# Settling transposes, two split slots and one set of low parts, moved in a transformer block on one core

## The chip, the core and the metric

The kernel runs on one core of a Trainium2 chip. The metric is the device time of one execution in microseconds (us); lower is better. A core has five engines that this text names: TensorE (PE in the profile; its weight loads are PEld), VectorE (DVE), ScalarE (ACT), GpSimd (POOL) and SyncE (SP, which issues DMAs here).

## What is computed

The reference is one block of a perceiver on 32 sequences of 64 tokens of 512 features, all in float32, with three residual layers. Cut to what matters here:

```python
x = x + xattn(layernorm(x), ctx_2048, mask)          # cross attention, 256 context tokens
x = x + attn(layernorm(x), wq_a, wq_b, wkv_a, wkv_b, wo, ...)   # latent attention, 16 heads
r = layernorm(x)
routing = top_k(r @ gate_w, 2)
h = square(relu(r @ up_w))                           # 512 -> 2048
y = h @ down_w + (r @ expert_weight) * routing.sum()
x = x + layernorm(y) * ln_gamma + ln_beta
```

## The kernel before, in words

A float32 product is made of three matmuls of a faster format: each operand is split into a high part `hi` (a rounded copy, made by ScalarE) and a low part `lo = x - hi` (made by VectorE), and hi*hi, hi*lo and lo*hi are added up in PSUM. `split` (L144) is that pair of instructions, and a `pins` argument tells behind which instructions the two are to be queued on their engines.

The three large products, `wo` (the attention's way out), `up` and `down`, use a recursive scheme that makes seven products of eight. For that, sums of weight blocks are made on GpSimd ahead of time (`prep_sums`) and stored in DRAM. Each large weight is cut into eight pieces, k = 0 to 7, used in the order `ORDER = (0, 1, 5, 6, 7, 2, 3, 4)`. Each has a slot in SBUF. `read_slot(k, what)` (L644) loads a piece of `wo`, `up` or `down` into its slot, and `put_slot(k, what, pins)` (L652) splits it there: two copies on ScalarE and two subtractions on VectorE, the first 1024 elements wide, the second 768.

The stages follow one another on TensorE. First come the cross attention and the latent attention (to about 550 us of the profiled execution). Then the way out (`seven`, L723 to L726, tile `op`) runs over eight token blocks of 256, with the expert's product (`o_expert`, tile `cpe`) and transposes (`o_t`, tile `ops`) of earlier blocks between. The way up (`up_seven`, matmuls on L1156, tile `up`) runs over four blocks of 512 tokens, b = 0 to 3, with eight rounds each, n = 0 to 7, one per weight piece; a round is 42 matmuls of 256 columns. The way down (`seven` again, tile `dp`) runs over units of a token block and a weight piece, u = 0 to 63, 21 matmuls each.

A round of the way up writes four PSUM banks. `combine` (L158 to L168) adds them up into a tile `uo`: a copy on ScalarE (L160) and five additions on VectorE, the last of which, L168, reads the last bank. Two sets of banks alternate, so round n + 2 needs the banks that round n's `combine` frees. Then ScalarE applies Relu and Square (L1226, L1227), and the result is stored in DRAM (`h_d`) and read back for the way down, where `left` splits it (tile `hl`).

The right operand of the way up is the features of a block, `xr[b, part]`. Parts 0 and 2 are high parts (copies on ScalarE, L1067) and parts 1 and 3 are the low parts of 0 and 2 (two subtractions on VectorE, L1065). `right(b, part)` makes one. For block 1 they are made in rounds of block 0: `PARTS_FIRST` maps m = n - 3 to the parts made at the end of that round.

`settle(n, ps, ...)` (L709) issues n transposes into a PSUM bank whose content isn't used. With `behind=None` nothing but the bank and their operands holds them back. In the way down four of them are chained behind the last matmul of the unit before (at the units in `SETTLE_AT`, L1359).

The order of the instructions on each engine is made when the program is built: a scheduler takes instructions in the order in which they are traced, as soon as a cost model says that they are ready, and `after(ins)` (`issue_after`) forces everything in its block behind `ins` on that engine. Memory that a closed pool leaves is given to the tiles of later pools, which wait until the earlier tile was last used. The pool `o_act` (tiles `beb`, `mo`, `xt`, `oo`, and others, in the order of their first allocation) gives its memory to the first tiles `uo` of the way up and to the rooms of the features behind them.

Of the kernel before, what the change touches and what calls it, by code (L numbers as in the profile page):

```python
# [9 lines left out]
FP = mybir.dt.float32  # L10
# [8 lines left out]
P = 128  # L19
B, S, D = 32, 64, 512  # L20
# [9 lines left out]
NB = (B * S) // TB  # L30
# [11 lines left out]
ORDER = (0, 1, 5, 6, 7, 2, 3, 4)  # L42
# [2 lines left out]


XR = "hxhx"
PARTS_FIRST = {1: (0, 1), 2: (2,)}
PARTS = {1: (0,), 2: (1,), 3: (2,)}

BARE_FIRST, BARE_LAST = ORDER[:5], ORDER[2:]
# [35 lines left out]
def perceiver_block(ctx: ExitStack, tc: tile.TileContext, x, mem, mask, wq_a, bq_a, qnw, wq_b, bq_b,  # L87
                    wkv_a, bkv_a, kvnw, wkv_b, wo, bo, gate, up, down, expert, gamma, beta, cs, out):
    nc = tc.nc
# [51 lines left out]
    def after(ins):  # L141
        return tc.issue_after(ins.ins) if ins is not None else ExitStack()
# [32 lines left out]
    def mm3(ps, pairs):  # L175

        n = len(pairs)
        for j, (ah, al, bh, bl) in enumerate(pairs):
            nc.tensor.matmul(ps, ah, bh, start=(j == 0), stop=False)  # L179
            nc.tensor.matmul(ps, al, bh, start=False, stop=False)  # L180
            nc.tensor.matmul(ps, ah, bl, start=False, stop=(j == n - 1))  # L181


    with ExitStack() as mla:
# [25 lines left out]
        with ExitStack() as pa:  # L210
# [304 lines left out]
            for i in range(NT + 2):  # L515
# [37 lines left out]
                if i < NT:  # L553
                    xT = a_xT(i)
# [446 lines left out]

    def o_expert(blk, xh, xl, _):

        mo = mos.pop(blk, None) or ap.tile([P, 2, D], FP, tag="mo", name=f"mo{blk}")
        for tt in range(2):
            i = 2 * blk + tt
            sl = slice(tt * P, (tt + 1) * P)
            pes = []
            for c in (slice(256, NE), slice(0, 256)):
                pe = ps_t.tile([P, D], FP, tag="T", name=f"cpe{i}_{c.start}")  # L1010
                mm3(pe[:, 0 : c.stop - c.start], [
                    (xh[:, k, sl], xl[:, k, sl], wes[0][:, k, c], wes[1][:, k, c]) for k in range(NKD)
                ])
                pes.append(pe)
            t8 = sp.tile([P, 8], FP, tag="t8", name=f"t8{i}")
            nc.vector.max(t8, pes[0][:, 256:264])
            gs = sp.tile([P, 1], FP, tag="gs", name=f"gs{i}")
            nc.vector.tensor_tensor(gs, t8[:, 0:1], t8[:, 1:2], ALU.add)
            if tt:
                yield  # L1020
            nc.scalar.mul(mo[:, tt, 256:512], pes[0][:, 0:256], gs)
            nc.scalar.mul(mo[:, tt, 0:256], pes[1][:, 0:256], gs)
        nc.scalar.dma_start(mo_d[blk], mo)
        yield

    xr, xc, xw = {}, {}, []

    def read_x(b, kk, room=None, behind=None):

# [37 lines left out]
                    ins = nc.scalar.copy(t[:, to], src)  # L1067
        return ins

    mos = {0: ap.tile([P, 2, D], FP, tag="mo", name="mo0")}  # L1070
    put_slot(ORDER[2], "wo")
    xt, xns, xT, x2s, dones, read = {}, {}, {}, {}, {}, 5
    for u, (blk, k) in enumerate(out_units):
# [61 lines left out]
    xT = o_t(NB - 1, xns.pop(NB - 1), lambda: next(scaled))  # L1135
    for part in range(3):
        right(0, part, (dones[NB - 1][0], xT[2][1]))
    put_slot(ORDER[2], "up", pins=xT[2])
    for _ in o_expert(NB - 1, *xT):
        pass  # L1140
    pc.close()


# [2 lines left out]
    with ExitStack() as pu:  # L1146
# [3 lines left out]
        def up_seven(ps, k, b, n, steps):  # L1150
            wh, wl = (t[:, 0:7].rearrange("p a (k f) -> p a k f", k=2) for t in wts[k])

            def product(s, parts, first=False, last=False):
                i, j = SEVEN[s]
                for m, (kk, w, low) in enumerate(parts):
                    nc.tensor.matmul(  # L1156
                        ps[s // 2][:, s % 2], w[:, i, kk], xr[b, 2 * kk + low][:, j],
                        start=(first and m == 0), stop=(last and m == len(parts) - 1),
                    )

            most = [(0, wh, 0), (0, wl, 0), (0, wh, 1), (1, wh, 0), (1, wl, 0)]
            rest = [(1, wh, 1)]
            one, two = (0, 2, 4, 6), (1, 3, 5)
            late = None
            if n == 0:
                with after(settle(8, ps, wh[:, 0, 0], ident2, None) if b == 0 else None):
                    for s in one:
                        product(s, most, first=True)
            if n == 7:
                for s in one:  # L1170
                    product(s, rest, first=True)
                for s in (0, 2, 4):
                    product(s, most, last=True)
                for s in two:
                    product(s, rest, first=True)
                if b + 1 < NB // 2:
                    late = right(b + 1, 3)
            for s in range(7):
                if n == 0 and s in one:
                    product(s, rest, last=True)  # L1180
                elif n < 7:
                    product(s, most + rest, True, True)
                elif s in two or s == 6:
                    product(s, most, last=True)
                if s in (1, 3, 5, 6):
                    with after(late if s == 3 else None):
                        next(steps)
# [8 lines left out]
                nc.sync.dma_start(h_d[b][:, k, 3:7], w)  # L1196

        stores = []
        right(0, 3)
        behind = read_slot(ORDER[5], "up", behind=reads[-1])  # L1200
        for b in range(NB // 2):
            if b == NB // 2 - 1:
                first = [(blk, k) for ks in (ORDER[:5], ORDER[5:]) for blk in DOWN[:2] for k in ks]
                out_units[:] = first + [(blk, k) for blk in DOWN[2:] for k in ORDER]
            for n, k in enumerate(ORDER):
                m = n - 3 if b == 0 else n - 1
                summed = None
                if 0 < b < NB // 2 - 1 and m in (0, 1):
                    read_x(b + 1, m)
                if b == 0 and n in (1, 2):  # L1210
                    behind = read_x(1, n - 1, x_room(1, n - 1), behind)
                if b == 0 and n in (0, 1):
                    behind = read_slot(ORDER[n + 6], "up", behind=behind)
                if b == NB // 2 - 1 and 0 < n < 7:
                    read_slot(ORDER[n - 1], "down")
                if b == NB // 2 - 1 and n == 4:
                    read_home(2, from_h, None)
                if b == NB // 2 - 1 and n in (5, 6):
                    read_pair(n - 2, from_h)
                ps = banks(ps_f[n % 2], f"up{b}_{k}")  # L1220
                o = fp.tile([P, 5, TB], FP, tag="o", name=f"uo{b}_{k}")
                p1 = fp.tile([P, TB], FP, tag="p1", bufs=2, name=f"up1_{b}_{k}")
                done = []
                up_seven(ps, k, b, n, combine(p1, ps, o, done))
                for q in (slice(0, 2), slice(2, 4)):
                    nc.scalar.activation(o[:, q], o[:, q], AF.Relu)  # L1226
                    act = nc.scalar.activation(o[:, q], o[:, q], AF.Square)  # L1227
                pins = (act, done[-1])
                o4 = o[:, 0:4].rearrange("p (c t) (a n) -> p c t a n", c=2, a=2)
                w = None  # L1230
                if not bare(b, k):
                    w = ccp.tile([P, 8, P], FP, tag="c", name=f"uw{b}_{k}").rearrange("p (d t) n -> p d t n", t=2)
                    at = [o4[:, i, :, a] for i in range(2) for a in range(2)] + [w[:, d] for d in range(4)]
                    summed = sums(at, LEFT)
                if b == 0 and n < 5:
                    put_slot(ORDER[n + 3], "up", pins=pins)
                if b == NB // 2 - 1 and 1 < n < 7:
                    put_slot(ORDER[n - 2], "down", pins=pins)
                if b == NB // 2 - 1 and n == 2:
                    for u in range(2):  # L1240
                        read_home(u, from_h, None)
                if b == NB // 2 - 1 and n == 3:
                    left(0, pins=(done[0], done[-1]))
                if b == NB // 2 - 1 and n == 5:
                    left(1, pins=(done[0], done[-1]))
                if b == NB // 2 - 1 and n == 6:
                    left(2, pins=(done[0], done[-1]))
                if b == NB // 2 - 1 and n == 7:
                    read_pair(5, from_h)
                if stores and (b, n) != (NB // 2 - 1, 7):  # L1250
                    store_h(*stores.pop(0))
                stores.append((b, k, o4, w))
                if b + 1 < NB // 2:
                    if m in (0, 1):
                        sum_x(b + 1, m, summed)
                    for q in (PARTS_FIRST if b == 0 else PARTS).get(m, ()):
                        right(b + 1, q, pins)

    with ExitStack() as pd:
# [82 lines left out]
        for u, (blk, k) in enumerate(out_units):  # L1342
# [23 lines left out]
                store_h(*stores.pop(0))  # L1366
            if u == 6:
                nc.sync.dma_start(gab, gamma.partition_broadcast(P))
            if u in (4, 6, 8):
                put_slot(ORDER[3 + u // 2], "down")  # L1370
            if u in (2, 4):
                read_slot(ORDER[5 + u // 2], "down")
            outs = [d for d in outs if step(d, low)]
# [52 lines left out]
```

## Time and profile before

| | us |
|---|---|
| median of 3 runs | 1103.69 |
| the three runs | 1099.43, 1103.69, 1105.27 |
| the profiled execution | 1098.9 |
| its span, first to last instruction | 1096.7 |
| its granted TensorE clock | 0.998 |

| engine | busy us | share of the span | instructions |
|---|---|---|---|
| PE | 1066.9 | 97% | 10201 |
| DVE | 769.0 | 70% | 1369 |
| ACT | 546.1 | 50% | 1051 |
| POOL | 508.1 | 46% | 691 |

The span is one execution, taken by the hardware profiler. In the timeline, a row is a start, a duration, an engine, a line of the kernel, an operation, the tiles written and read, their shapes and a count of merged instructions; in square brackets stands how long the engine had been idle and what ended that. In a table of windows a row is a stretch, its length, the busy time of the engine with the number of instructions, the granted clock, the mean busy share of the DMA engines and the GB/s that they moved. Matmuls overlap: one lasts 0.28 us and the next starts before it ends.

### The profile page before, as it was taken

The page shows a single profiled execution, that of the slowest core. Times are in us where ns is not written, and L with a number is a line of the kernel's source. Part 1 is how long each engine was busy: PE and PEld are TensorE (multiplying, and loading weights), DVE is VectorE, ACT ScalarE, POOL GpSimd, SP SyncE. Part 2 cuts the span into 40 slices and gives each one's busy share as a digit, 9 for nine tenths or more (in the row PEclk, how much of TensorE's full clock was granted, in tenths as well). Part 3 has the DMA queues.
Part 4 walks back from the last instruction along what each step waited for, and adds up shares of the span by engine and source line. Part 5 has one row for each costly group of instructions (what it writes and reads, how often), then busy time and mean ns, then how long its engine had stood idle before and what let it go on. Part 6 is the DMA issues. An engine that isn't in the chain of part 4 may idle for free.

```text
span 1096.7 us, 26072 instructions
## 1 busy us (share of the span) xinstructions
PE 1066.9 (97%) x10201; PEld 983.6 (90%) x10201; DVE 769.0 (70%) x1369; ACT 546.1 (50%) x1051; POOL 508.1 (46%) x691
## 2 busy tenths in 40 slices
PE   8999999999999999999998999999999999999996
PEld 6667777679999999999988999999999999999996
DVE  5666666657666666656787866667785658898786
ACT  4444444533433444434475544445676567755553
POOL 2333333326788778874570000003238970065671
PEclk9999999999999999999999999999999999999999
DMA  8867666343776778655487776779646689998672
GB/s 259 263 216 231 206 212 203 124 161 121 260 234 245 260 247 294 249 207 195 160 324 276 263 241 213 231 235 359 218 156 202 221 247 366 310 309 257 206 232 79
DMA packets 195386, 254.67 MB, mean 232 GB/s; under 512 B 18544, under 2 KB 140032, under 8 KB 195264
## 3 DMA queue, kind: packets, MB, share of 16 engines
q1 hardware_dynamic: 190704, 240.92, 67.0%
q10 hardware_dynamic: 3456, 8.39, 2.2%
q0 software_dynamic: 1104, 3.70, 0.9%
q8 instruction: 80, 1.31, 0.5%
q14 instruction: 42, 0.34, 0.1%
HBM read 146.67 MB, written 106.30 MB: 231 GB/s over the span
## 4 chain that ended last, share of the span: by engine, by line
PE 59%; DMA 10%; POOL 9%; DVE 8%; issue 7%; ACT 5%; SPq 1%; DVEq 0%; POOLq 0%; ACTq 0%
PE up L1156 9%; PE pss L773 5%; PE psq L179 4%; PE psq L180 4%; PE psq L181 4%; PE op L725 3%; PE op L726 3%; PE op L723 3%; PE psv L817 3%; DMA hd<-uo 2%; PE pse L179 2%; PE pse L181 2%; PE pse L180 2%; DMA x1d<-xt 2%; DMA vd<-vw 2%
## 5 line engine op out<-in xcount | busy, mean ns | idle before, releaser
L755 DVE SCALAR_TENSOR_TENSOR qe<-pse,bqp,cq 64x256 f32<-64x256 f32 x256 | 123.7, 483 | 76.5 <-PE pse L181 70.7
L1156 PE MATMUL up<-xr,wh_up 128*128 128x256 f32 x896 | 157.6, 280 | 0.6 <-DVE uo L168 0.6
L1156 PEld LDWEIGHTS up<-xr,wh_up 128*128 128x128 f32 x896 | 137.5, 189 | 1.0 <-issue 0.7
L725 PE MATMUL op<-wh_wo,hl 128*128 128x256 f32 x448 | 124.4, 279 | 3.7 <-DVE hl L149 3.7
L723 PE MATMUL op<-wh_wo,hl 128*128 128x256 f32 x448 | 124.0, 280 | 0.6 <-ACT hl L147 0.6
L725 PE MATMUL dp<-wh_down,hl 128*128 128x256 f32 x448 | 124.5, 278 | 0.0
L723 PE MATMUL dp<-wh_down,hl 128*128 128x256 f32 x448 | 124.4, 278 | 0.0
L726 PE MATMUL dp<-wl_down,hl 128*128 128x256 f32 x448 | 124.3, 277 | 0.0
L149 DVE TENSOR_TENSOR hl<-c,hl 128x896 fp32r<-128x896 f32 x84 | 94.3, 1126 | 42.3 <-ACT hl L147 42.0
L1156 PE MATMUL up<-xr,wl_up 128*128 128x256 f32 x448 | 123.7, 280 | 0.0
L726 PE MATMUL op<-wl_wo,hl 128*128 128x256 f32 x448 | 123.5, 277 | 0.0
L147 ACT CAST hl<-c 128x896 fp32r<-128x896 f32 x84 | 79.0, 942 | 77.7 <-PE op L726 38.0
L179 PE MATMUL psq<-qa_hi,qh 128*128 128x256 f32 x384 | 112.5, 293 | 0.0
L180 PE MATMUL psq<-qa_hi,ql 128*128 128x256 f32 x384 | 106.4, 277 | 0.0
L181 PE MATMUL psq<-qa_lo,qh 128*128 128x256 f32 x384 | 106.2, 276 | 0.0
L725 PEld LDWEIGHTS op<-wh_wo,hl 128*128 128x128 f32 x448 | 84.3, 188 | 4.8 <-DVE hl L149 4.7
L723 PEld LDWEIGHTS op<-wh_wo,hl 128*128 128x128 f32 x448 | 83.6, 188 | 1.5 <-ACT hl L147 0.8
L723 PEld LDWEIGHTS dp<-wh_down,hl 128*128 128x128 f32 x448 | 84.6, 189 | 0.0
L725 PEld LDWEIGHTS dp<-wh_down,hl 128*128 128x128 f32 x448 | 84.1, 188 | 0.4 <-DVE hl L149 0.4
L1156 PEld LDWEIGHTS up<-xr,wl_up 128*128 128x128 f32 x448 | 84.2, 188 | 0.0
L726 PEld LDWEIGHTS op<-wl_wo,hl 128*128 128x128 f32 x448 | 84.1, 188 | 0.0
L726 PEld LDWEIGHTS dp<-wl_down,hl 128*128 128x128 f32 x448 | 84.1, 188 | 0.0
(233 smaller groups left out, 3146.6 us busy)
## 6 DMA issues: line engine op xcount, KB each, us to landing
c<-vd SPq DMA_DIRECT2D x58, 448.0 KB, 4.2
cx<-in_ctx SPq DMA_DIRECT2D x32, 512.0 KB, 4.6
vd<-vw SPq DMA_DIRECT2D x29, 512.0 KB, 3.6
hd<-uo SPq DMA_DIRECT2D x107, 128.0 KB, 3.3
hd<-uw SPq DMA_DIRECT2D x21, 512.0 KB, 3.3
dcw<-hd SPq DMA_DIRECT2D x18, 448.0 KB, 5.6
vd<-v SPq DMA_DIRECT2D x30, 256.0 KB, 3.5
wd_wo<-pw_wo SPq DMA_DIRECT2D x8, 896.0 KB, 4.9
```

The source lines that it names most:

```text
L147: copy = nc.scalar.copy(hi, src)
L149: return copy, engine.tensor_tensor(lo, src, hi.bitcast(FP), ALU.subtract)
L179: nc.tensor.matmul(ps, ah, bh, start=(j == 0), stop=False)
L180: nc.tensor.matmul(ps, al, bh, start=False, stop=False)
L181: nc.tensor.matmul(ps, ah, bl, start=False, stop=(j == n - 1))
L723: first = nc.tensor.matmul(ps[s // 2][:, s % 2], h[:, a], wh[:, b], start=(k == 0 and s % 2 == 0), stop=False)
L725: nc.tensor.matmul(ps[s // 2][:, s % 2], l[:, a], wh[:, b], start=False, stop=False)
L726: ins = nc.tensor.matmul(ps[s // 2][:, s % 2], h[:, a], wl[:, b], start=False, stop=last)
L755: rope = nc.vector.scalar_tensor_tensor(qe[64 * a : 64 * a + 64, :], pe[r, :], bqp[r, p : p + 1], cq[r, a, :], ALU.add, ALU.mult,)
L773: nc.tensor.matmul(ps[64 * j : 64 * j + 64, pj, b, :], qs[2 * pj + j][a][:, sl], kT[:, a, kt], start=(a == 0), stop=(a == 1),)
L817: nc.tensor.matmul(o, kv[a, i, :], t[a, bp, :], start=True, stop=True)
L1156: nc.tensor.matmul(ps[s // 2][:, s % 2], w[:, i, kk], xr[b, 2 * kk + low][:, j], start=(first and m == 0), stop=(last and m == len(parts) ...
```

## The change

Five edits:

- The settling transposes ahead of the way up are four instead of eight, and they are pinned behind the last matmul of the last expert product (`ends`, for which `mm3` now returns its last matmul).
- `mo`, the expert's result, is no longer allocated ahead of the loop, so its place in `o_act` comes behind the tiles that are allocated earlier.
- `put_slot(ORDER[2], "up")` moves from before the last expert product to behind `right(0, 3)`, with its subtractions pinned behind that. `put_slot(ORDER[3], "up")` moves from the end of round 0 to the same place.
- In the last block of the way up, `put_slot(ORDER[4], "down")` moves from the end of round 6 to unit 0 of the way down, pinned behind the last Square and the last L168 of the way up.
- Block 1's part 1 (the low parts of its first features) is made at the end of round 5 of block 0 instead of round 4.

```diff
-PARTS_FIRST = {1: (0, 1), 2: (2,)}
+PARTS_FIRST = {1: (0,), 2: (1, 2)}
...
-            nc.tensor.matmul(ps, ah, bl, start=False, stop=(j == n - 1))
+            ins = nc.tensor.matmul(ps, ah, bl, start=False, stop=(j == n - 1))
+        return ins
...
-        mo = mos.pop(blk, None) or ap.tile([P, 2, D], FP, tag="mo", name=f"mo{blk}")
+        mo = ap.tile([P, 2, D], FP, tag="mo", name=f"mo{blk}")
...
-                mm3(pe[:, 0 : c.stop - c.start], [
+                made.append(mm3(pe[:, 0 : c.stop - c.start], [
                     (xh[:, k, sl], xl[:, k, sl], wes[0][:, k, c], wes[1][:, k, c]) for k in range(NKD)
-                ])
+                ]))
...
-    xr, xc, xw = {}, {}, []
+    xr, xc, xw, made = {}, {}, [], []
...
-    mos = {0: ap.tile([P, 2, D], FP, tag="mo", name="mo0")}
     put_slot(ORDER[2], "wo")
...
-    put_slot(ORDER[2], "up", pins=xT[2])
     for _ in o_expert(NB - 1, *xT):
         pass
+    ends = made[-1]
     pc.close()
...
-                with after(settle(8, ps, wh[:, 0, 0], ident2, None) if b == 0 else None):
+                with after(settle(4, ps, wh[:, 0, 0], ident2, ends) if b == 0 else None):
...
-        right(0, 3)
+        put_slot(ORDER[2], "up", pins=(xT[2][0], right(0, 3)))
+        put_slot(ORDER[3], "up", (xT[2][0], None))
...
-                if b == 0 and n < 5:
+                if b == 0 and 0 < n < 5:
                     put_slot(ORDER[n + 3], "up", pins=pins)
-                if b == NB // 2 - 1 and 1 < n < 7:
+                if b == NB // 2 - 1 and 1 < n < 6:
                     put_slot(ORDER[n - 2], "down", pins=pins)
...
-            if u in (4, 6, 8):
-                put_slot(ORDER[3 + u // 2], "down")
+            if u in (0, 4, 6, 8):
+                put_slot(ORDER[max(4, 3 + u // 2)], "down", pins=pins if u == 0 else (None, None))
```

## The prediction

> **What bounds the kernel now.** I read the page first: engines, then the granted clock.
>
> ```profile
> PE 1066.9 (97%) x10201; PEld 983.6 (90%) x10201; DVE 769.0 (70%) x1369; ACT 546.1 (50%) x1051; POOL 508.1 (46%) x691
> ...
> PEclk9999999999999999999999999999999999999999
> ```
>
> TensorE (PE) is busy for 97% of the span and the granted clock is full in every slice, so only two things can move the end: gaps in PE's stream, and the distance from one matmul's start to the next. A "busy" PE hides the second, since matmuls overlap. So I counted instructions in stretches of 20 us in the middle of the way up (windows, PE alone).
>
> ```profile
> 785.00:805.00 20.00, 20.00 (x172) 1.00 0.45 126
> 815.00:835.00 20.00, 20.00 (x179) 1.00 0.72 237
> 860.00:880.00 20.00, 20.00 (x172) 1.00 0.66 220
> ```
>
> All are 100% busy at clock 1.00, with the same matmuls (L1156, 256 columns), yet one holds 179 and the others 172. A matmul lasts 0.28 us, so some 2.4 of the count are the overlap at the edges: 20/176.5 is 113.3 ns apart, 20/169.7 is 117.8. The starts in the timeline say the same everywhere behind 560 us: 113.33 or 117.78 ns, nothing between for long. I call them the quick and the slow pace; 4.45 ns apart, 3.8% of PE time. Following the starts, the slow stretches behind 560 us are 560-576, 585-611, 773-809, 847-943 and 1036-1065 us. The pace changes only where PE is interrupted. At 808.87:
>
> ```profile
> 808.87 0.48 PE L1156 MATMUL up<-xr,wh_up 128*128 128x256 f32 x2 [0.57 <-DVE uo L168]
> ```
>
> slow before, quick after. Three late starts at 846.8-847.5 (258, 242 and 222 ns) do the reverse. Of the waits whose after-pace can be read, about as many end quick as slow. A row of transposes is another matter: each row of eight (L985) from 625 to 744 us and each row of four settling ones (L713, at 943.5 out of the slow pace, at 1008.3 out of the quick) is followed by the quick pace. Ahead of the way up:
>
> ```profile
> 764.82 1.08 PE L985 MATMUL ops<-ident,on 128*128 128x128 f32 x8 [1.02 <-DVE on L139]
> 765.75 0.49 PE L713 MATMUL up<-ident,wh_up 128*128 128x128 f32 x3
> 766.66 0.51 PE L179 MATMUL cpe<-we_hi,oh 128*128 128x264 f32 x2 [0.43 <-ACT oh L147]
> 767.01 0.60 PE L713 MATMUL up<-ident,wh_up 128*128 128x128 f32 x4
> ...
> 773.04 0.27 PE L713 MATMUL up<-ident,wh_up 128*128 128x128 f32 x1
> 773.07 0.36 PE L1156 MATMUL up<-xr,wh_up 128*128 128x256 f32 x1
> ```
>
> Seven of the eight settling transposes run ahead of the expert's matmuls; one stands where it was meant, and the way up starts slow. Last, VectorE (DVE) ahead of the stall at 808.87, and its hole at the start of the way up:
>
> ```profile
> 780.10 0.69 DVE L162 TENSOR_TENSOR uo<-up,up 128x512 f32<-128x512 f32 x1 [4.67 <-ACT up L160]
> ...
> 804.29 2.10 DVE L149 TENSOR_TENSOR wl_up<-wl_up,wh_up 128x1024 fp32r<-128x1024 f32 x2 [0.32 <-ACT wh_up L147]
> 806.30 0.96 DVE L1065 TENSOR_TENSOR xr<-xp,xr 128x768 fp32r<-128x768 f32 x1
> 807.17 1.23 DVE L1065 TENSOR_TENSOR xr<-xc,xr 128x1024 fp32r<-128x1024 f32 x1
> 808.30 0.42 DVE L168 TENSOR_TENSOR uo<-uo,up 128x256 f32<-128x256 f32 x1
> ```
>
> L168 frees the last bank of the sixth weight of block 0; the eighth weight needs it four matmuls after its start. It is late because the low part of block 1's features (L1065, 2.1 us) stands ahead of it. In the five rounds before, one round of DVE is five combining steps (2.6 us) and two low halves of a slot (2.1 us): 4.73 us from one L168 to the next (787.38, 792.11, 796.84, 801.57). A round of 42 matmuls takes 4.95 us slow and 4.76 quick: at the quick pace DVE has no room.
>
> **The change, part by part**, against the profiled execution's 1098.9 us (span 1096.7).
>
> *Pinned transposes.* Eight become four in a row behind the last expert matmul. Three of the eight lay in PE's 0.43 us wait and cost nothing; five stood on the path; now four do, at 109 ns: -0.1 us. If the row works as the rows at 625-744, 943.5 and 1008.3 did, the 302 matmuls from 773.07 to 808.87 come 4.45 ns closer: -1.35 us. Nothing is queued behind the pin but the way up itself, which needs the expert's end anyway.
>
> *Features' low parts apart.* The two L1065 move one round later, behind L168 and away from a slot's low halves. The stall's starts were 851 and 194 ns after their predecessors instead of 113: -0.82 us. They are needed where block 1 starts, some 811 us; behind L168 of the sixth round they end near 809. ScalarE's (ACT's) part of that round (L1067, 1.9 us) does not move. Next late would be L168 of the seventh round, pushed by 2.1 us; its bank is needed a whole round later, so it is covered.
>
> *One slot more ahead; rooms.* ORDER[3]'s split (ACT 1.8 us, DVE 2.1 us) leaves DVE's first round and goes to 770-774, where ACT is free until the scaling at 772.57 and DVE waits for the expert's last matmul before right(0, 3). ORDER[2]'s low halves go behind right(0, 3), into the hole that ends at 780.10; they are due at 782.6. Both slots landed before 767 us and the puts issue no DMA, so the SP and POOL queues keep their order. Behind ACT's two extra casts stand the expert's scalings and their store, at most 1.8 us later. That store mattered: mo's room lay under the first `uo`, and it landed at 779.97, just before L162 at 780.10, though its matmuls were done near 777.1. With mo allocated last, that room is that of tiles done earlier, and the first combine starts up to 2.8 us sooner. PE did not wait for it (bank due at 783.0), so 0 now; this pays for the quick pace: without it the rounds' 4.73 us would run into 4.76 us. If the cover failed, one stall like the present one, 0.8 us, and the pace open again.
>
> *One slot in the way down.* ORDER[4]'s split leaves 933.8-937.0 and goes behind the last Square and the last L168. Without its casts (1.67 us of ACT) ahead, the last Square ends at 938.6 instead of 940.2, or a us sooner if the casts of hl step behind it; then casts 1.77 us and the last low half 1 us: 940.3 to 941.4. The way down's fifth unit, which multiplies by it, is due at 931.05 + 84 x 0.1178 = 940.95. Behind it on both engines stand units' hl and slots ORDER[5], ORDER[6]; the low of the seventh unit ended at 946.3, when PE took it. So the price lies between 0 and about 2 us in small stalls; I take +0.4, nearer the low end, since DVE's own L168 comes 2 us earlier for it and both engines' work in that stretch stays the same.
>
> *Behind 809.* In the profiled execution 809-847 was quick already: 0 there. But all three timed runs (1099.43 to 1105.27) lie above the profiled one, so a typical run has more slow stretches; half of 38 us x 3.8% is -0.65 for the median run. The waits at 846.8 come from POOL's sums and the later right parts of block 1, which the change does not touch; I expect them again, with the pace afterwards open.
>
> Sum for a median run: -0.1 - 1.35 - 0.82 - 0.65 + 0.4 = -2.5 us, on 1103.69: **1101.2**. On the profiled execution, without the half, -1.9: 1097.0.
>
> [...]
>
> **Rivals.** (1) *All of the way up quick.* The waits at 847 vanish or come out quick, and block 2's likewise. Block 2 took 39.57 us, block 3 39.46, where 336 x 113.33 is 38.08: -2.87; block 1's tail -0.17; the way down's first 105 matmuls -0.47. With -2.5 that is -6.0: 1097.7; on the profiled run, with -1.9, -5.4: 1093.5. For it: block 1 ran quick for seven rounds. Against: its eighth round stalled just at that pace, and each stall is a coin.
>
> (2) *The row does nothing here*, or a stall in the first rounds undoes it. Then only -0.1 - 0.82 + 0.4: with no stall at 808.87 nothing brings the quick pace back, and 38 us of block 1 turn slow, +1.4 on the profiled run. So +0.9 for a run whose block 1 was quick and -0.5 for one where it was slow already, +0.2 between them: 1103.9. For it: the one row of four at 557.5 was slow again three us later, after a wait.
>
> (3) *Slower: the late split at the head of the way down.* ACT is full from 931.7 to 945.4. If ORDER[4]'s casts come out behind the seventh unit's cast (943.49, 0.94 us), they end at 946.2, the low half at 947.3, and the fifth unit waits 6.3 us; the units behind it then find their operands late, and the pace after the settling is lost until 1008 (62 us x 3.8% = 2.3). -2.5 - 0.4 + 6.3 + 2.3 = +5.7: 1109.4. It decides from a wait of some 3 us on. For it: the pin on the last Square; against: the split is traced ahead of that cast.
>
> **How the numbers follow.** Forecast case 0.45, rival 1 0.25, rival 2 0.15, rival 3 0.15. A measurement here tells about 0.5%, 5.5 us. The runs scatter by some 3 us on either side, from pace alone. Faster by more: 0.2 of the forecast case, 0.8 of rival 1, 0.1 of rival 2: 0.31. Slower by more: 0.05, none, 0.1, 0.9: 0.17. The rest, 0.52, is no change. The range reaches from below rival 1 (1097.7 less the scatter, and the profiled run's 1093.5) to rival 3's 1109.4: 1093 to 1109.
>
> **What the changed profile would show.** Right: four L713 in one row behind the last cpe, starts of L1156 113.33 ns apart from there, 179 matmuls in 785-805; no wait near 806; L162 of the first round near 777.3; ORDER[3]'s low halves before right(0, 3); the split of ORDER[4] done by 941 and no PE wait over 0.3 us in the fifth unit. Wrong: 172 in that window; a wait for `xr` or a slot in the first four rounds; a wait of PE for wl_down at the fifth unit. What I can't see is how the four changed orders shift the scheduling of each engine elsewhere; a stall in a place that I took as untouched would break the sum.

## The result, and the profile after

The median of 20 runs is 1105.18 us (1102.85 to 1109.99); the kernel before, run beside it, has 1102.24 us over 20 runs. The ratio is 1.0035, 95% interval [1.0021, 1.0049]: slower by 3.9 us of 1102.24 (the two medians differ by 2.9), where 2.5 us less was forecast. The profiled execution of after is the slowest of its 20 (1109.99 us, span 1108.2), that of before was one of the fastest of its kernel (1098.9), so the two traces differ by more than the medians do; what follows from a trace alone is said so. In the experiments one execution, the profiled one of the first kernel with the late place alone, took 3691.59 us with its matmuls some 0.41 us apart; its trace is not read, and that kernel was run a second time.

On the page, PE is as busy as before and the clock looks full (`PEclk` has a digit for each of 40 slices of the span):

```profile
PE 1072.0 (97%) x10197; PEld 986.5 (89%) x10197; DVE 770.3 (70%) x1369; ACT 545.3 (49%) x1051; POOL 508.0 (46%) x691
PEclk9999999999999999999999999999999999999998
```

PE has four instructions less and 5.1 us more of busy time. The three windows of the way up (PE alone; start and end, length, busy time with the count, clock, DMA share, GB/s) show where the count is lost:

```profile
785.00:805.00 20.00, 19.76 (x168) 1.00 0.38 107
815.00:835.00 20.00, 17.09 (x132) 0.91 0.66 216
860.00:880.00 20.00, 20.00 (x172) 1.00 0.65 211
```

The first window should have had 179 and has 168; the second had 179 before and has 132, with PE idle for 2.9 us and the clock cut. Ahead of the way up, in the timeline of PE:

```profile
764.83 1.08 PE L986 MATMUL ops<-ident,on 128*128 128x128 f32 x8 [0.94 <-DVE on L139]
766.67 0.51 PE L179 MATMUL cpe<-we_hi,oh 128*128 128x264 f32 x2 [0.75 <-ACT oh L147]
767.39 0.46 PE L180 MATMUL cpe<-we_hi,ol 128*128 128x264 f32 x1 [0.22 <-DVE ol L149]
...
774.54 0.60 PE L714 MATMUL up<-ident,wh_up 128*128 128x128 f32 x4
774.89 0.37 PE L1156 MATMUL up<-xr,wh_up 128*128 128x256 f32 x1
```

The row of four stands where it was meant, and from the third on the starts of L1156 behind it are 113 to 115 ns apart. But the seven free transposes no longer fill the waits, and the way up starts 1.82 us later (773.07 before). The windows of PE tell how, before first, then after:

```profile
767.00:771.00 4.00, 4.00 (x35) 1.00 1.03 392
```

```profile
767.00:771.00 4.00, 3.78 (x19) 0.57 0.99 374
```

For one stretch of 3.41 us (767.56 to 770.98) the granted clock is half, and the expert's matmuls are some 220 ns apart instead of 120. VectorE at the start of the way up:

```profile
775.65 1.76 DVE L1066 TENSOR_TENSOR xr<-xc,xr 128x1024 fp32r<-128x1024 f32 x1
777.33 6.25 DVE L149 TENSOR_TENSOR wl_up<-wl_up,wh_up 128x1024 fp32r<-128x1024 f32 x4
783.50 0.67 DVE L162 TENSOR_TENSOR uo<-up,up 128x512 f32<-128x512 f32 x1
```

All four low halves of the two slots stand ahead of the first combining step, which comes at 783.50, not 780.10 as before and not 777.3 as forecast. From there VectorE and ScalarE handle two rounds at a time. One row of each engine's timeline shows them waiting for each other:

```profile
791.08 2.09 DVE L149 TENSOR_TENSOR wl_up<-wl_up,wh_up 128x1024 fp32r<-128x1024 f32 x2 [2.88 <-ACT wh_up L147]
```

```profile
795.18 1.16 ACT L1227 ACTIVATE uo<-uo 128x512 f32<-128x512 f32 x2 [2.88 <-DVE uo L166]
```

VectorE combines two rounds, ScalarE squares both and only then casts the next slot, VectorE waits for that cast to make its low halves, and ScalarE waits for the next pair. Two rounds take 11.04 us (L162 at 793.09 and at 804.13), 5.52 us a round, where PE needs 4.76. So PE runs into it, 0.65 us in the seventh round of block 0 and 2.91 us in the first of block 1:

```profile
805.41 0.36 PE L1156 MATMUL up<-xr,wh_up 128*128 128x256 f32 x1 [0.65 <-DVE up L163]
818.10 0.36 PE L1156 MATMUL up<-xr,wh_up 128*128 128x256 f32 x1 [2.91 <-DVE uo L162]
```

Right behind the second, from 818.76 to 822.18, the clock is half again, and the slow pace follows to 950. From the first L1156 to the second round of block 1 the kernel takes 49.75 us, against 45.07 before. In the way down, where PE before waited for nothing, the fifth unit waits now (and the eighth, 0.74 us twice):

```profile
948.83 0.38 PE L724 MATMUL dp<-wh_down,hl 128*128 128x256 f32 x1 [0.35 <-ACT hl L147]
950.38 0.38 PE L726 MATMUL dp<-wh_down,hl 128*128 128x256 f32 x1 [1.17 <-DVE hl L149]
```

### The profile page after: what moved, and what is told of

The parts are those of the page before. It is cut to its first block, busy times and chain, and to the rows that moved or that the text cites. A ratio compares the mean times of both kernels' runs of the same rounds, so it can differ in the third digit from the quotient of the medians.

```text
span 1108.2 us, 26062 instructions
## 1 busy us (share of the span) xinstructions
PE 1072.0 (97%) x10197; PEld 986.5 (89%) x10197; DVE 770.3 (70%) x1369; ACT 545.3 (49%) x1051; POOL 508.0 (46%) x691
## 4 chain that ended last, share of the span: by engine, by line
PE 63%; DVE 9%; issue 8%; POOL 8%; DMA 7%; ACT 4%; SPq 0%; DVEq 0%; POOLq 0%; ACTq 0%
PE up L1156 12%; PE pss L774 6%; PE psq L179 4%; PE psq L180 4%; PE psq L181 4%; PE op L726 3%; PE op L727 3%; PE op L724 3%; PE psv L818 3%; DMA c<-hd 2%; PE psc L374 2%; PE pse L179 2%; PE pse L181 2%; PE pse L180 2%; DMA c<-vd 2%
## 5 line engine op out<-in xcount | busy, mean ns | idle before, releaser
L1156 PE MATMUL up<-xr,wh_up 128*128 128x256 f32 x896 | 159.4, 282 | 3.7 <-DVE uo L162 2.9
L1156 PEld LDWEIGHTS up<-xr,wh_up 128*128 128x128 f32 x896 | 138.9, 191 | 4.2 <-issue 4.2
L1156 PE MATMUL up<-xr,wl_up 128*128 128x256 f32 x448 | 124.8, 282 | 0.0
L1156 PEld LDWEIGHTS up<-xr,wl_up 128*128 128x128 f32 x448 | 85.0, 190 | 0.3 <-DVE wl_up L149 0.2
```

The costliest lines, as they stand in the source:

```text
L1156: nc.tensor.matmul(ps[s // 2][:, s % 2], w[:, i, kk], xr[b, 2 * kk + low][:, j], start=(first and m == 0), stop=(last and m == len(parts) ...
```

## The experiments

The theories have letters in the expectations. A: without the free transposes the clock is halved ahead of the way up, and that is the loss. C: the slot splits ahead of the way up are (C1 the one slot more, C2 its place behind `right(0, 3)`). D: the moved features' low parts are. E: the late split in the way down is. P: the row sets the pace. R: `mo`'s room pays. Ratios are to the kernel before, run beside each; "faster" or "slower" means that the whole 95% interval lies on one side of 1, and every difference here is below 1%; "row" is the four pinned transposes with the eight free ones taken out, "split" the features' low parts one round later, "room" `mo` without its early place.

**Four single edits.** The row alone, on the kernel before (with the lines that make `ends`):

```diff
-                with after(settle(8, ps, wh[:, 0, 0], ident2, None) if b == 0 else None):
+                with after(settle(4, ps, wh[:, 0, 0], ident2, ends) if b == 0 else None):
```

> The kernel before with one edit: four settling transposes pinned behind the last expert matmul instead of eight free ones. Theory A (the free transposes were what kept PE active through its wait for oh near 766 us; without them the clock is halved for one window of 3.4 us): a halved window near 767.5 us, cpe matmuls 220 ns apart in it, the way up starts 1.8 us later (some 774.9 us instead of 773.07), then at the quick pace (113 ns) up to the stall near 809; net with -1.35 us for the pace: 0 to +1 us against before. Rival B (the clock drop in the changed kernel comes from its other edits on ScalarE and VectorE): no halved window, the way up starts within 0.3 us of before, net -1.3 us or more.

Measured: 1102.87 us, 0.9992 [0.9973, 1.0011]. The halved clock is there (768.4 to 771.9); the way up starts quick, turns slow in the last round of block 0 and stays so to 943.

The kernel after, with the eight free transposes given back ahead of the four:

```diff
+                if b == 0:
+                    settle(8, ps, wh[:, 0, 0], ident2, None)
                 with after(settle(4, ps, wh[:, 0, 0], ident2, ends) if b == 0 else None):
```

> The changed kernel with the eight free transposes put back ahead of the four pinned ones. Theory A: no halved window near 767 us, the way up starts at 773.5 us (before's 773.07 plus the four pinned), so 1 to 1.5 us less than the changed kernel; the waits in block 0 of the way up and at the head of the way down stay. Rival B: the halved window stays, and the time is that of the changed kernel plus 0.3 us.

Measured: 1107.29 us, 1.0031 [1.0008, 1.0054]. The clock is whole through the expert's matmuls, and it doesn't help; the late wait stays as it was:

```profile
820.96 0.36 PE L1156 MATMUL up<-xr,wh_up 128*128 128x256 f32 x1 [2.92 <-DVE uo L162]
```

The kernel after, with both splits of the way up where they were in before:

```diff
+    put_slot(ORDER[2], "up", pins=xT[2])
     for _ in o_expert(NB - 1, *xT):
...
-        put_slot(ORDER[2], "up", pins=(xT[2][0], right(0, 3)))
-        put_slot(ORDER[3], "up", (xT[2][0], None))
+        right(0, 3)
...
-                if b == 0 and 0 < n < 5:
+                if b == 0 and n < 5:
```

> The changed kernel with ORDER[2]'s and ORDER[3]'s splits of the way up put back where they were before (the rest as changed). Theory C (both slots' low halves stand ahead of the first combine on VectorE, so VectorE and ScalarE run late through block 0, and block 1's first round waits 2.9 us, with a second halved window): the first L162 comes near 780 instead of 783.5, no wait over 1 us at block 1's first round, no halved window there, 3 to 5 us less than the changed kernel. Rival D (the wait at block 1's first round comes from the moved low parts of the features, L1066): the wait stays and the time is within 1 us of the changed kernel.

Measured: 1099.93 us, 0.9971 [0.9948, 0.9994]: faster than before. First L162 at 777.75, no wait in blocks 0 and 1, the quick pace in every round up to a wait of 0.44 us in the sixth round of block 3 (912.65) and the slow one behind it, though the clock is halved from 765.8 to 769.2. The halved clock of A is there and is not the loss, D falls (the moved L1066 is still there), C holds.

The kernel after, with `ORDER[4]`'s split of the way down at the end of round 6 again:

```diff
-                if b == NB // 2 - 1 and 1 < n < 6:
+                if b == NB // 2 - 1 and 1 < n < 7:
...
-            if u in (0, 4, 6, 8):
-                put_slot(ORDER[max(4, 3 + u // 2)], "down", pins=pins if u == 0 else (None, None))
+            if u in (4, 6, 8):
+                put_slot(ORDER[3 + u // 2], "down")
```

> The changed kernel with ORDER[4]'s split of the way down put back to round 6 (the rest as changed). Theory E (the late split is why the way down's fifth to eighth units wait, 1.5 + 1.1 + 1.0 + 0.7 us in the profile of the changed kernel): those waits are gone, 2 to 4 us less than the changed kernel. Rival F (those units wait because the way up's late ScalarE and VectorE queues reach into the way down, whatever is split there): the waits stay in another unit and the time changes by less than 1 us.

Measured: 1106.6 us, 1.0021 [0.9997, 1.0044]. The fifth unit's waits are gone and the waits of blocks 0 and 1 are not (0.65 us at 807.70, 2.55 us near 820.4): E isn't the loss either.

**Both groups of splits put back**, the row, the split and the room kept:

> The kernel after with all slot splits put back as before, those of the way up and the ORDER[4] split of the way down; the pinned row, the features' split and the new room of mo stay. Theory A+C+E (the late split costs the way down some 1 to 2 us by its own): way up as with the way-up splits alone put back (first L162 near 777.8, 113.33 ns in blocks 0 and 1, no wait there), and the waits of 1.2 us in the fifth unit gone: 1.0 to 2 us below the 1099.9 us of that kernel, some 1098.5, ratio to before 0.995 to 0.997. Rival (the late split costs nothing when the way up is on time, since a wait moves to another unit): 1099.5 to 1100.5, with a wait of 0.4 to 1 us in units 0 or 6 instead.

Measured: 1099.75 us, 0.9969 [0.9949, 0.9989], with way up quick to block 2's last round and no wait in the fifth unit. Of the 1 to 2 us that E expected nothing is seen beside the 1099.93 of the kernel before it.

**The same as the third kernel, with the eight free transposes ahead of the row:**

> The kernel after with the way-up slot splits put back as before, and the eight free settling transposes given back ahead of the four pinned ones. Theory A (without work in the expert's waits the clock is halved for 3.4 us there, and the way up starts some 1.7 us later): no halved stretch between 765 and 772, the expert's matmuls 120 ns apart, way up starting near 773.2 instead of near 775, everything behind it as in the kernel without the free ones; 1.0 to 1.7 us below its 1099.9 us, some 1098.6. Rival (the halved stretch comes in some 3 to 5 places of a run anyway and only moves to another): same time within 0.5 us, with a halved stretch elsewhere in the way up or the way down.

Measured: 1102.49 us, 0.9993 [0.9974, 1.0011]. No halved clock through the last expert's matmuls (it is halved some 10 us earlier, from 756.55 to 763.37), yet not faster. In its trace the first round has two late starts (170 and 225 ns) near 781.2, where the second part of `right(0, 3)` ended at 781.16, and from there the pace is slow. PE came sooner and met an operand that was not ready. Whether that costs the 2.7 us between the two medians can't be told from one trace.

**The features' split alone:**

```diff
-PARTS_FIRST = {1: (0, 1), 2: (2,)}
+PARTS_FIRST = {1: (0,), 2: (1, 2)}
```

> The kernel before with the features' low parts (the two L1065 of block 1) one round later and nothing else changed. Theory (the prediction's term): the wait of 0.57 us at 808.9 goes, the seven free transposes stay, the way up starts slow (117.78 ns) and with no wait nothing brings the quick pace: -0.8 us on block 0, up to +1.4 on block 1 if it stays slow: 1102 to 1103.5, ratio 0.999 to 1.001. Rival D (the moved right part stalls PE wherever it stands, as in the kernel after at 818): a wait of 0.5 to 3 us at the start of the seventh or eighth round, 1103 to 1106.

Measured: 1103.14 us, 0.9997 [0.9978, 1.0015]. The wait at 808.87 is gone; two late starts (143 and 226 ns) come at 820 instead and turn the pace slow. The way up doesn't start slow, as was expected: from its sixth start on it is quick. Its VectorE shows what holds the first combining step:

```profile
784.74 0.69 DVE L162 TENSOR_TENSOR uo<-up,up 128x512 f32<-128x512 f32 x1 [3.18 <-DMA mod<-mo]
```

It waits for the DMA that stores `mo` in DRAM (`mod`), 6.65 us behind the first L1156 (778.09).

**The kernel after, with both splits ahead of the last expert product:**

```diff
+    put_slot(ORDER[2], "up", pins=xT[2])
+    put_slot(ORDER[3], "up", pins=xT[2])
     for _ in o_expert(NB - 1, *xT):
...
-        put_slot(ORDER[2], "up", pins=(xT[2][0], right(0, 3)))
-        put_slot(ORDER[3], "up", (xT[2][0], None))
+        right(0, 3)
```

> The kernel after with both slot splits traced ahead of the last block's expert (where before had the first one alone) instead of behind right(0, 3). Theory C1 (one slot more ahead of the way up is the cause, wherever it stands: its low halves put DVE a round behind and the combining steps go two rounds at a time): first L162 at 780 or later, pairs of rounds on DVE, a wait of 2 us or more near the first round of block 1, time 1104 to 1107. Rival C2 (only the place behind right(0, 3) is bad): first L162 near 778, no wait in blocks 0 and 1, time near 1100.

Measured: 1107.25 us, 1.0031 [1.0008, 1.0054]. First L162 at 783.13, rounds in pairs (L162 at 793.39 and 804.44), and the wait again:

```profile
818.88 0.45 PE L1158 MATMUL up<-xr,wh_up 128*128 128x256 f32 x1 [2.51 <-DVE uo L162]
```

Here two low halves stand ahead of the second part of `right(0, 3)` and PE waits 1.67 us for it in the first round (782.30), so the first L162 is late for PE's sake. The pairs come all the same.

**The late place without the slot more:** after, with `ORDER[3]`'s line deleted and `n < 5` again, so that only `ORDER[2]`'s split stands behind `right(0, 3)`.

> The kernel after with ORDER[3]'s split given back to the first round of the way up; ORDER[2]'s stays behind right(0, 3). One of the two edits to the way up's splits alone: the place without the one slot more. On VectorE the two low halves of ORDER[2] then stand between right(0, 3) and the first L162, and from there the order is that of the kernel with both splits put back. Theory C1 (one slot more ahead is the cause): first L162 near 780 to 781, rounds combined one by one, no wait of 2 us or more at the start of block 1, time 1100 to 1102. Rival C2 (the place behind right(0, 3) is enough): a wait near 818 of some 2.5 us as in the kernel after, 1104 to 1107.

> The kernel of the late place without the one slot more again, for a trace in which TensorE runs as in all others. Theory C1 (one slot more ahead makes VectorE combine two rounds at a time): first L162 right behind two low halves near 780 to 782, from there one round at a time, no wait of 1 us or more in blocks 0 and 1, median 1101 to 1102. Rival C2 (the place behind right(0, 3)): a wait of 2 us or more between 815 and 825.

Measured: 1101.65 us, 0.9982 [0.9963, 1.0002] and, again, 1100.42 us, 0.9966 [0.9952, 0.9981]. VectorE in the second:

```profile
775.01 3.18 DVE L149 TENSOR_TENSOR wl_up<-wl_up,wh_up 128x1024 fp32r<-128x1024 f32 x2
778.11 0.68 DVE L162 TENSOR_TENSOR uo<-up,up 128x512 f32<-128x512 f32 x1
...
783.38 2.09 DVE L149 TENSOR_TENSOR wl_up<-wl_up,wh_up 128x1024 fp32r<-128x1024 f32 x2
785.39 0.42 DVE L168 TENSOR_TENSOR uo<-uo,up 128x256 f32<-128x256 f32 x1
```

Two low halves ahead instead of four; from the second round on each round's low halves lie between its L166 and its L168, one round at a time, and PE doesn't wait in blocks 0 and 1. C1 holds, C2 falls. The kernels with one slot and with two differ in that put alone: 1.0035 / 0.9982 and 1.0035 / 0.9966 are 1.0053 and 1.0069, 6 to 8 us (4 to 6 us by the medians, each less that of the kernel before beside it). The order itself says the same: VectorE's instructions from the first L162 on stand in pairs of rounds in all four kernels with two slots ahead, and in single rounds in all eleven others whose trace can be read. That order is made when the program is built; why the scheduler turns to pairs was not looked into.

**What pays: pairs of the row, the split and the room, on the kernel before.** The room's edit:

```diff
-        mo = mos.pop(blk, None) or ap.tile([P, 2, D], FP, tag="mo", name=f"mo{blk}")
+        mo = ap.tile([P, 2, D], FP, tag="mo", name=f"mo{blk}")
...
-    mos = {0: ap.tile([P, 2, D], FP, tag="mo", name="mo0")}
```

> The kernel before with the pinned row and the features' split; mo keeps its first room and all slot splits stay as before. Against the kernel with the room moved as well (1099.75 us). Theory R (the room matters: with mo under the first uo the first L162 waits for the expert's store, VectorE has no slack at the quick pace, and a short wait of PE in block 0 or at the start of block 1 ends it): first L162 6 us or more behind the first L1156, the quick pace lost before 825, 1101.5 to 1103. Rival R0 (the prediction's 0 for the room): first L162 late but PE never waits for it, quick pace through block 1, 1099.5 to 1100.5.

> The kernel before with the features' split and mo's new room, without the pinned row (the eight free settling transposes stay). Theory P (the row sets the pace): way up starts slow at 117.78 ns, or quick only after a wait in its first round; no wait at the start of block 1 with either; 1102 to 1103.5. Rival P0 (the split and the room alone free the stream and the row is not needed): quick through blocks 0 to 2, 1099.5 to 1100.5. The settling transposes should again keep the clock whole between 755 and 775.

> The kernel before with the pinned row and mo's new room, the features' low parts left in the sixth round. Theory D2 (the two L1065 in that round hold L168 back and the quick pace ends there, as with the row alone): quick to the sixth round of block 0, then a wait or two late starts between 800 and 812 and slow behind them, 1101.5 to 1103. Rival D0 (with the first combine on time VectorE has room for the low parts where they were): quick through block 1, 1099.5 to 1100.5, and the split of the features is worth nothing.

> The kernel before with mo's new room and nothing else changed. Theory R (the room is the part that pays: the first combine no longer waits for the expert's store, so VectorE enters the rounds 2 us and more earlier and absorbs the features' low parts): first L162 4.2 to 4.8 us behind the first L1156 instead of 6.7 to 7, no wait near 808 to 820 although L1065 stands where it was, 1100 to 1101.5, ratio 0.9965 to 0.9985. Rival R0 (the room only lets the row or the split work and is worth nothing by itself): 1102.5 to 1103.5, ratio 0.999 to 1.001.

| kernel | median us | ratio |
|---|---|---|
| row | 1102.87 | 0.9992 [0.9973, 1.0011] |
| split | 1103.14 | 0.9997 [0.9978, 1.0015] |
| row and split | 1101.61 | 0.9990 [0.9972, 1.0007] |
| room | 1099.27 | 0.9968 [0.9954, 0.9983] |
| row and room | 1099.97 | 0.9970 [0.9947, 0.9994] |
| split and room | 1101.20 | 0.9976 [0.9958, 0.9994] |
| row, split and room | 1099.75 | 0.9969 [0.9949, 0.9989] |

Each of the four with the room is faster than before, none of the three without is; what the row and the split add to the room is less than the runs can tell. (The kernel above with the way-up splits put back and twelve transposes has the room too and is not faster; its pace turned slow in the first round.) The traces put the gain into the way up: from its first matmul to its last they have 155.0 to 158.7 us in the five kernels without the room, 153.9 to 155.9 in six with it and 158.3 in that one, and 158.9 to 163.4 in the four with two slots ahead. With row and split but without the room the first L162 comes 6.82 us behind the first L1158 (783.36 and 776.54), and PE waits 0.40 us at 815.28, as R had it. VectorE with the room alone:

```profile
780.93 0.69 DVE L162 TENSOR_TENSOR uo<-up,up 128x512 f32<-128x512 f32 x1 [1.35 <-PE up L1155]
...
807.82 0.95 DVE L1065 TENSOR_TENSOR xr<-xp,xr 128x768 fp32r<-128x768 f32 x1
808.69 1.22 DVE L1065 TENSOR_TENSOR xr<-xc,xr 128x1024 fp32r<-128x1024 f32 x1
809.83 0.41 DVE L168 TENSOR_TENSOR uo<-uo,up 128x256 f32<-128x256 f32 x1
```

The first combining step now waits for PE, 4.84 us behind the first L1155 (776.09), where before it came 7.03 us behind (780.10 less 773.07) and waited for the store. The profile puts that wait of before down to L160, which ended at 780.09. But in all five traces with the first room L162 starts 0.12 or 0.13 us behind the landing of the store (779.97 in before), and in the seven with the new room and no slot more it starts 0.5 to 2.8 us ahead of it. The 2.19 us between are about the length of the two L1065 (2.1 us): they stand ahead of L168 as before, and now nothing is late, the most that PE shows there being starts of 124 and 116 ns. With the first room the lag depends on when the store lands: 4.94 us with the row alone, 5.74 to 7.03 us in the other four. What else moves in memory with `mo` was not tested apart. In its windows all three stretches are quick:

```profile
785.00:805.00 20.00, 20.00 (x179) 1.00 0.42 119
815.00:835.00 20.00, 20.00 (x179) 1.00 0.78 258
860.00:880.00 20.00, 20.00 (x179) 1.00 0.75 248
```

The row is not there, and the starts are 113 or 114 ns apart from the sixth on, 0.7 us into the way up, ahead of the wait of 0.32 us for the features in the first round (779.63). It is so in four of the five traces that keep the eight transposes alone; the profiled before, slow from its second start, is the exception. R holds, P and D2 fall.

**The late split in the way down alone**, on the kernel before:

> The kernel before with ORDER[4]'s split of the way down moved behind the last unit of the way up, and nothing else changed. Theory E1 (the late split stalls the fifth and the following units): a wait of 1 us or more in units 4 to 6, 1104 to 1105.5, ratio 1.001 to 1.002. Rival E0 (it fits into the slack there; the prediction's +0.4): waits as before, 1102.5 to 1103.6, ratio 0.9995 to 1.0008.

Measured: 1104.48 us, 1.0007 [0.9992, 1.0021]; one wait in the fifth unit that before has not:

```profile
946.53 0.39 PE L725 MATMUL dp<-wh_down,hl 128*128 128x256 f32 x1 [1.11 <-DVE hl L149]
```

The wait is E1's, the ratio between the two; it is small either way. In the traces all seven kernels with the late split wait 0.75 to 1.73 us in the fifth unit and none of the nine without it does, but six of these nine wait 0.31 to 1.17 us in the seventh.

## Why the prediction was wrong, point by point

- **The step that failed is "One slot more ahead; rooms", and in it both terms.** It placed `ORDER[3]`'s split at 770 to 774, "where ACT is free until the scaling at 772.57", and `ORDER[2]`'s low halves in the hole that ends at 780.10. Traced behind the expert, the casts stand behind the expert's scalings (775.84 to 777.62), the low halves behind `right(0, 3)` (774.74 and 775.65), and beside GpSimd's sums they take 1.75 and 1.49 us instead of 1.23 and 0.95. So two slots' 4.2 us of low halves became 6.25 us, in a hole that was 4.67 us long and that the first combining step was to end earlier. The prediction gave 0, or one stall of 0.8 us if the cover failed. What it didn't think of is that the order of the later rounds changes as well: rounds go in pairs, at 5.52 us against PE's 4.76, and the lag grows until a wait of 2.9 us. The price is 6 to 8 us by the ratios. Less the room's 3.5 and with the late split's 0.8 that is some 3 to 5 us, and 3.9 was measured. That 1105.18 lies within the stated 1093 to 1109 is luck: the upper part of that range was there for rival 3, another cause.
- **The room was sized at 0 and pays about 3.5 us** (0.9968 of 1103). The mechanism was named: L162 held by `mo`'s store, first combine "up to 2.8 us sooner" (2.2 measured). The mistake was to value it by PE's next wait. In before, VectorE's late entry ran through all rounds of block 0 and was one with the wait at 808.87, as the room alone shows.
- **Features' low parts, -0.82: the reading was right, the worth was not.** The L1065 were ahead of the late L168, as said, but they only showed the lag. Moved alone, they make PE late at 820 instead: the 27th matmul of block 1 starts 0.05 us behind the second L1065 of part 3 (818.58, 1.22 us), which stands behind the seventh round's late L168. With the row as well (without the room), PE waits 0.40 us at 815.28 for that round's own steps, where the prediction wrote "so it is covered".
- **Transposes: one trace was taken for the rule.** Behind the row the pace was quick within 0.7 us in all its kernels; one of the two with twelve transposes left it after 3 us. But the slow start, which the -1.35 was to end, is in one of five traces with the eight alone. The -1.35 and -0.65 can't be seen: -0.9 us for the row alone, from -3.0 to 1.2. "Three of the eight lay in PE's 0.43 us wait and cost nothing; five stood on the path" was wrong as well: without the free ones PE waits 0.75 and 0.22 us there. From the last row of eight (L985 or L986) to the first matmul of the way up it is 8.21 to 8.25 us in the five traces with the eight alone, 8.56 to 8.58 in five with the row, and 9.88 to 10.06 in four with the row and a halved clock there. So the row costs 0.3 us where -0.1 was put down, and of the 1.82 us in the profiled pair some 1.5 are the clock's. Of the nine kernels without the free transposes whose trace can be read, those four had a halved clock in the last expert's stretch (some 764 to 778), two had it some 10 us earlier, three had none near; of the seven with them none had it there, three some 10 us earlier. The medians show no gain from keeping them, so their worth beyond one trace is open.
- **Transposes and the clock.** In the last expert's stretch the clock was halved in none of the seven traces with the free transposes and in four of the nine without them: that leans to the side that they keep it whole there, and doesn't settle it.
- **Late split, +0.4: in its range.** 0.8 us measured, interval -0.9 to 2.3. Rival 3's place was right and its price (6.3 and 2.3 us) was not.
- **What was marked as wrong came in part**: 172 or less in 785 to 805 (168); a wait in the third round (0.10 us at 784.78), but for a bank and not for `xr` or a slot; and one in the fifth unit, but for `hl` and not for the slot. The closing remark, that shifted orders elsewhere would break the sum, is what happened, a few us behind the edit rather than elsewhere.
- **Two slips in the sum**: 297 matmuls, not 302, lie between 773.07 and 808.87, and half of 38 us x 3.8% is 0.72, not 0.65. The sum would be -2.6.
- **Against what**: the profiled before lay 3 to 5 us below the median of the runs beside each kernel, and its clock is whole up to 1091 us; the median after must be set against 1102 to 1103 us.

The version to keep is the kernel before with the room alone: 1099.27 us, 0.9968 of before where the changed kernel has 1.0035. Other kernels with the room are level with it.

## What to carry to other kernels

When several engines turn in a loop behind a bounding one, read how late the helper enters the loop, and what its first step waits for; a late wait seven rounds on may be that lag, and a change of which tile takes whose memory can remove it for nothing (here the 0.57 us at 808.87, gone with the room alone). A pace or a wait that a single trace shows may be the exception: look for it in several traces before it is priced. Work put "into a hole" ahead of a loop must be placed by what the engine's queue has in front of it, and with the durations that it has beside other engines (here 6.25 us for four low halves that take 4.2 with GpSimd idle); then look at the order that the loop itself takes behind it, since one item more in stock can turn an overlapped round into two engines waiting for each other in turn (here 5.52 us a round against PE's 4.76).

## What the runs showed of the hardware

- VectorE's subtractions took longer beside GpSimd's sums: 1024 columns took 1.22 us with GpSimd idle (770.99 of before) and 1.75 to 1.76 us within its sums (775.65, 777.33 and 780.42 of after), 768 columns 0.95 and 1.49 us (772.47 of before, 779.00 of after). A pair of GpSimd's sums took 3.39 us beside them (776.28 of after) and 1.55 us with VectorE idle (776.69 of before).
- In the profiled execution of after the clock fell to half for 3.41 us (from 767.56) after PE had been idle for 1.9 us in three pieces (0.94, 0.75 and 0.22 us) between 764 and 767.6. In three other traces with 1.8 to 1.9 us in the same pieces it stayed whole. Behind the long wait at the start of block 1 it fell in three kernels (2.91, 2.92 and 2.51 us) and not in the fourth (2.55 us).
- In these traces the 256-column matmuls of the way up kept one of two distances, 113.33 or 117.78 ns, at full clock (179 or 172 of them in 20 us at clock 1.00, in before and with both splits ahead of the last expert product), for 100 us and more at a stretch. The distance changed at short waits, in either direction (0.27 us at 780.24 turned it slow with the late split alone, 0.57 us at 808.87 quick in before); what decides was not found.
